# Queries of a self attention by seven block products of 128 tokens instead of eight

## The chip, the cores and the metric

One core of a Trainium2 chip runs the whole program in one launch. The metric is the device time of one execution in microseconds (us); several executions are timed and the median is given. A profile is one further execution taken with the hardware profiler; its times are from its own first instruction.

## What is computed

Sixteen elements of 256 tokens by 256 channels go through two transformer blocks. Each block has a self attention, a cross attention and a feed-forward part. All numbers are 32-bit floats. The change concerns the self attention of the first block (layer 0), cut here to what matters:

```python
def _attn(xq, ctx, wq, wkv, wo, bo):       # xq = ctx = adaptive layer norm of x, 256 tokens x 256
    q = _heads(xq @ wq)                    # wq: 256 x 1024, 16 heads of 64
    k, v = jnp.split(ctx @ wkv, 2, axis=-1)
    k = _heads(k)
    v = _heads(v)
    q = _rope(q, sq, cq)                   # rotary turn of each pair of channels
    k = _rope(k, sk, ck)
    sim = jnp.einsum('bhnd,bhmd->bhnm', q, k) * DH ** (-0.5)
    a = jax.nn.softmax(sim, axis=-1)
    o = jnp.einsum('bhnm,bhmd->bhnd', a, v)
    return o.transpose(0, 2, 1, 3).reshape(xq.shape[0], xq.shape[1], MID) @ wo + bo
```

## The kernel before

**Order.** The kernel writes out the instruction order of every engine by hand: what is called first stands first in each engine's queue. Six phases follow each other (layer 0 self, cross, feed-forward; the same for layer 1), each a loop over the 16 elements ("jobs"; `job["b"]` is the element, `job["p"]` the phase, 0 for the one changed). An attention job has two steps, s = 0 and s = 1. In each step two groups `u` = 2s and 2s + 1 of four heads are worked on. Step by step the kernel makes the queries and keys of the *next* step (`then`), the weighted sums of this one, and closes with `scores(i + 1)`: the products of queries and keys of the next step (`stage_s`, L657) into the eight PSUM banks, from which ScalarE takes the exponentials `pr` (L670).

**Products.** `product` (L82) is one 128 x 128 weight block times a moving operand, sent as four matmuls of 32 output columns. The trace keeps two records of each such matmul, so a product is eight records.

**Queries and keys before.** `stage_rotary` makes half a group: two products with 256 moving tokens for the keys and two for the queries, side by side in one bank. VectorE multiplies that bank by cosine and by sine (L614, tiles `m`), and after the second half GpSimd adds and subtracts the products (L622, tiles `qk`, 512 columns each for queries and keys together). A step has eight query products and eight key products. The four calls use banks 0, 1, 2 and 3 in turn.

**Values by seven.** The values of elements 2 to 15 are made in step s = 0 of the element before by seven block products in place of eight (a Strassen scheme in its Winograd form: two blocks of input channels by two blocks of tokens, and the same of the weights). `fold_tokens` (L532 to L535) makes the four sums of the input's blocks on GpSimd, `fold_value_weights` those of the weights, once. `value_part` puts the seven products (L82, 512 columns) into banks 4, 6 and 7 and collects them with ScalarE copies and VectorE additions: part 0 makes two products and copies bank 6 to bank 7 (L551); part 1 makes one product in bank 6 and one in bank 7 and copies both out (L555, L556); part 2 makes one more in bank 7, copies it out (L559) and adds on VectorE (L560); part 3 one in bank 7 (L563); part 4 one in bank 4 and an addition (L566).

**Around it.** `stage_t` (L676) adds the exponentials of two halves on VectorE, both inputs in SBUF; `stage_turn` (L682) and `stage_reduce` (L689) sum them over keys; `sum_up` makes the reciprocals and sends them through DRAM to `spread`. `layer0_sums` (L724) are the weighted sums of values, copied out by ScalarE (L731). On GpSimd `scale` (L713) multiplies them by the reciprocals and `fold_inner` (L1003) makes sums for the output product, `finish_folded`, which is 28 products of 128 moving columns (L82, operands `folded`, `raw`, `folded_w`, `wo_sa`), in step s = 1. The order of one step s = 0 with the values by seven was:

```python
rotary(then, 0, 0); rotary(then, 0, 1); sum_up(late, 5)
value_part(nxt, 0); stage_t(job, 1); stage_reduce(job, 0)
rotary(then, 1, 0); value_part(nxt, 1)
rotary(then, 1, 1); value_part(nxt, 2)
layer0_sums(job, 0, 5); value_part(nxt, 3)
layer0_sums(job, 1, 6); stage_turn(job, 1); value_part(nxt, 4); stage_reduce(job, 1)
```

Of the kernel before, what the change touches and what calls it, by code (L numbers as in the profile page):

```python
# [10 lines left out]
F32 = mybir.dt.float32  # L11
# [5 lines left out]
P = 128  # L17
# [26 lines left out]
def fast(ctx: ExitStack, tc: tile.TileContext, a: dict, out: bass.AP, flag):  # L44
# [19 lines left out]
    def bank(i, *inner):  # L64

        flat = banks[:, i, :]
        if len(inner) == 1:
            return flat[:, 0 : inner[0]]
        return flat[:, 0 : inner[0] * inner[1]].rearrange("p (a n) -> p a n", n=inner[1])
# [443 lines left out]
    def fold_value_weights(ph, eng):  # L513

        wv = ph["w"]["wv"]
        top, low = ([wv[:, k, r * 512 : (r + 1) * 512] for k in range(KC)] for r in range(2))
        sums = wtile([P, 4, 512], "wo", "sums_of_weights", 2)
        s2, s3, s4 = (sums[:, i] for i in range(3))
        eng.tensor_tensor(s3, top[0], low[0], ALU.subtract)
        eng.tensor_tensor(low[0], low[0], low[1], ALU.add)  # L520
        eng.tensor_tensor(s2, low[0], top[0], ALU.subtract)
        eng.tensor_tensor(s4, top[1], s2, ALU.subtract)
        ph["value_weights"] = {1: top[0], 2: top[1], 3: s4, 4: low[1], 5: low[0], 6: s2, 7: s3}

    def fold_tokens(job, eng):

        b = [[job["hT"][:, k, t * P : (t + 1) * P] for t in range(NT)] for k in range(KC)]
        t1, t2, t3, t4 = (
            tile[:, i, :] for tile in
            [wtile([P, 2, P], "bv", f"tokens{i}_{job['key']}", 2) for i in range(2)] for i in range(2)  # L530
        )
# [4 lines left out]
        job["tokens"] = {1: b[0][0], 2: b[1][0], 3: b[1][1], 4: t4, 5: t1, 6: t2, 7: t3}  # L536

# [3 lines left out]
    def value_part(job, part):  # L541
# [15 lines left out]
        elif part == 2:  # L557
            value_product(job, 7, 7)
            nc.scalar.copy(low2, chain)  # L559
            nc.vector.tensor_tensor(low2, bank(4, 512), low2, ALU.add)  # L560
        elif part == 3:
            value_product(job, 4, 7)
            nc.scalar.copy(low, chain)  # L563
        else:
            value_product(job, 3, 4)
            nc.vector.tensor_tensor(top2, bank(4, 512), top2, ALU.add)  # L566
# [604 lines left out]
    for i, (j, s) in enumerate(steps):  # L1171
# [123 lines left out]
        elif layer0:  # L1295
            then = attention(i + 1, 0)
            if leaving and s == 1 and nxt["kind"] == "ffn":
# [4 lines left out]
            if s == 0 and by_seven(nxt):  # L1302
# [14 lines left out]
                value_part(nxt, 2)  # L1317
                layer0_sums(job, 0, 5)
# [41 lines left out]
            else:  # L1360
                prepare_norm(third)
                prepare_context(third)
                prepare_input(after)
                if job["b"] == 0:
# [651 lines left out]
```

## Time and profile before

| what | value |
|---|---|
| five timed executions, median | 2162.98 us (2161.99 to 2165.33) |
| profiled execution: its time, its span | 2161.8 us, 2159.9 us |
| granted TensorE clock | 1.000 |
| TensorE matmuls busy | 2141.4 us, 50000 records |
| VectorE, ScalarE, GpSimd busy | 1654.6, 877.8, 1321.9 us |
| one element of the self attention, from scores to scores (184.73 to 225.18 us) | 40.45 us, TensorE busy for all of it |
| in that element: VectorE, ScalarE, GpSimd busy | 30.87, 13.30, 29.61 us |

Times are us from the start of the span unless marked ns. PE is TensorE's matmul side, PEld its weight loads, DVE VectorE, ACT ScalarE, POOL GpSimd. In the timeline a line has start, length, engine, source line, operation, output and inputs, and how many instructions were merged; in brackets the idle time before, and what ended it. A merged matmul line is longer than its share of TensorE, since matmuls overlap their successors: the distance between starts is what a group costs.

### The profile page before, as it was taken

The numbers are of one execution on the slowest core, as the hardware profiler recorded it, in microseconds if no ns is written. First come the engines' busy times: TensorE is split into PE (matmuls) and PEld (weight loads), VectorE is DVE, ScalarE is ACT, GpSimd is POOL, SyncE is SP. The second block draws the span as 40 slices with busy tenths as digits, with TensorE's granted clock in tenths as the row PEclk, the third lists the DMA queues.
The fourth block names the chain that finished last, engine by engine and source line by source line (L and its number), as shares of the span: only waits on it lengthen the run. The fifth ranks groups of instructions, "written<-read, shape, count | busy, mean of one in ns | idle before, by whom it ended". The sixth has DMA issues, their size and how long they took to land.

```text
span 2159.9 us, 109747 instructions
## 1 busy us (share of the span) xinstructions
PE 2141.4 (99%) x50000; PEld 1409.7 (65%) x50000; DVE 1654.6 (77%) x3008; ACT 877.8 (41%) x1376; POOL 1321.9 (61%) x1234
## 2 busy tenths in 40 slices
PE   9999999999999999999999999999999999999998
PEld 5666666666666666666666667887556556656787
DVE  6777777777787888888888777764777777778875
ACT  3333333333323332333323333443666666664442
POOL 5767767767767877686776766661322223236673
PEclk9999999999999999999999999999999999999999
DMA  5110010110133221211212023220211232223221
GB/s 195 26 42 23 25 41 22 25 41 23 29 84 93 74 60 35 58 44 44 58 35 60 26 75 93 52 50 22 64 41 43 53 95 63 60 49 81 70 66 39
DMA packets 307027, 117.65 MB, mean 54 GB/s; under 512 B 243364, under 2 KB 289784, under 8 KB 306424
## 3 DMA queue, kind: packets, MB, share of 16 engines
q1 hardware_dynamic: 306008, 110.02, 20.1%
q8 instruction: 393, 6.44, 1.2%
q14 instruction: 82, 0.67, 0.1%
q10 hardware_dynamic: 544, 0.52, 0.1%
HBM read 77.14 MB, written 33.29 MB: 51 GB/s over the span
## 4 chain that ended last, share of the span: by engine, by line
PE 95%; POOL 2%; DVE 1%; SPq 1%; DMA 1%; issue 1%; ACT 0%; POOLq 0%; DVEq 0%; ACTq 0%
PE banks L82 60%; PE banks L657 16%; PE banks L724 10%; PE banks L740 5%; PE banks L593 2%; PE banks L502 1%; POOL folded L926 0%; POOL folded_w L994 0%; POOL qk L622 0%; SPq L389 0%; DVE m L614 0%; SPq L379 0%; DVE xh L364 0%; POOL x L452 0%; DMA rows<-in_rows 0%
## 5 line engine op out<-in xcount | busy, mean ns | idle before, releaser
L670 ACT ACTIVATE pr<-banks 128x1024 f32<-128x1024 f32 x576 | 487.3, 938 | 422.9 <-PE banks L657 218.7
L622 POOL TENSOR_TENSOR qk<-m,m 128x512 f32<-128x512 f32 x256 | 378.7, 1500 | 213.3 <-DVE m L614 205.8
L614 DVE TENSOR_TENSOR m<-banks,rope 128x512 f32<-128x512 f32 x512 | 319.7, 678 | 35.0 <-PE banks L82 24.9
L676 DVE TENSOR_TENSOR both<-pr 128x1024 f32<-128x1024 f32 x128 | 170.0, 1328 | 104.0 <-ACT pr L670 102.0
L657 PE MATMUL banks<-qk 32*64 32x256 f32 x8192 | 239.4, 377 | 0.8 <-POOL qk L622 0.5
L724 PE MATMUL banks<-pr,v 128*32 128x256 f32 x4096 | 235.8, 379 | 0.0
L731 ACT COPY raw<-banks 128x512 f32<-128x512 f32 x128 | 75.1, 586 | 390.6 <-PE banks L724 384.6
L657 PEld LDWEIGHTS banks<-qk 32*64 32x64 f32 x8192 | 184.4, 131 | 59.9 <-issue 26.0
L724 PEld LDWEIGHTS banks<-pr,v 128*32 128x32 f32 x4096 | 133.4, 110 | 100.1 <-issue 16.8
L782 POOL TENSOR_TENSOR oT<-oT,spread 128x256 f32<-128x256 f32 x64 | 45.7, 736 | 206.7 <-DVE spread L781 206.7
L713 POOL TENSOR_TENSOR raw<-raw,spread 128x512 f32<-128x512 f32 x128 | 162.6, 1304 | 13.7 <-DMA spread<-sums_seen 13.5
L682 DVE STREAM_TRANSPOSE squares<-both 128x1024 f32<-128x1024 f32 x128 | 158.8, 1240 | 2.2
L689 DVE TENSOR_REDUCE rows<-squares 128x32 f32<-128x1024 f32 x128 | 155.2, 1212 | 1.7
L452 POOL TENSOR_TENSOR x<-x,bo_b 128x256 f32<-128x256 f32 x96 | 72.8, 778 | 121.6 <-DVE xh L364 121.6
L1003 POOL TENSOR_TENSOR folded<-raw,raw 128x512 f32<-128x512 f32 x90 | 142.9, 1615 | 2.4
L82 PE MATMUL banks<-hT,wk_sa 128*32 128x256 f32 x2048 | 134.7, 381 | 0.4 <-ACT hT L422 0.4
L740 PE MATMUL banks<-pr,wide_v 128*32 128x256 f32 x2048 | 134.4, 379 | 0.0
L82 PE MATMUL banks<-hT,wq_ca 128*32 128x256 f32 x2048 | 134.0, 379 | 0.0
L82 PE MATMUL banks<-hT,wq_sa 128*32 128x256 f32 x2048 | 133.9, 379 | 0.0
L356 POOL TENSOR_TENSOR rstd<-ve,neg_half 128x2 f32<-128x2 f32 x95 | 67.6, 712 | 101.5 <-DVE ve L354 97.7
L657 PE MATMUL banks<-q,k 32*64 32x256 f32 x4096 | 128.3, 381 | 0.2 <-issue 0.2
L957 DVE TENSOR_TENSOR x<-banks,x 128x256 f32<-128x256 f32 (+2 forms) x150 | 79.6, 531 | 62.6 <-PE banks L82 56.4
(246 smaller groups left out, 4044.8 us busy)
## 6 DMA issues: line engine op xcount, KB each, us to landing
turned<-blocks SPq DMA_DIRECT2D x380, 64.0 KB
fetched<-turned SPq DMA_DIRECT2D x380, 64.0 KB
spread<-sums_seen SPq DMA_DIRECT2D x128, 128.0 KB
x<-in_x SPq DMA_DIRECT2D x16, 256.0 KB
fetched_c<-turned_c SPq DMA_DIRECT2D x64, 64.0 KB
cT<-in_ctx_turned SPq DMA_DIRECT2D x16, 256.0 KB
out<-x SPq DMA_DIRECT2D x15, 256.0 KB
ctx<-in_ctx SPq DMA_DIRECT2D x16, 192.0 KB
```

What stands on the lines that cost most here:

```text
L82: nc.tensor.matmul(out[cut], lhsT[:, cut], rhs, start=start, stop=stop, **more)
L614: nc.vector.tensor_tensor(m, pq, rope[:, s : s + 1, :].to_broadcast([P, 2, N]), ALU.mult)
L622: nc.gpsimd.tensor_tensor(r, x, y, (ALU.subtract, ALU.add)[out])
L657: nc.tensor.matmul(banks[64 * g : 64 * g + 64, at + h, t * N : (t + 1) * N], lhs, rhs, start=(half == 0 and (t == 0 or job["layer"] == 1)) ...
L670: nc.scalar.activation(pr[:, one], sc[:, one], AF.Exp, scale=0.125 if job["layer"] == 0 else 0.25)
L676: nc.vector.tensor_tensor(both, pr[:, :, 0, :], pr[:, :, 1, :], ALU.add)
L682: nc.vector.transpose(job["squares"].rearrange("p b k -> p (b k)"), job.pop("both").rearrange("p h n -> p (h n)"))
L689: nc.vector.tensor_reduce(job["rows"][:, u, :], job.pop("squares"), AX.X, ALU.add)
L713: nc.gpsimd.tensor_tensor(part, part, spread[:, u : u + 1, :].to_broadcast([P, 2, N]), ALU.mult)
L724: nc.tensor.matmul(o[32 * h : 32 * h + 32, half, :], v[:, t, col : col + 32], pr[:, h, t, :], start=(t == 0), stop=(t == NT - 1),)
L740: nc.tensor.matmul(o[32 * h : 32 * h + 32], v[:, t, 4 * c + h, 32 * e : 32 * e + 32], pr[:, h, t, :], start=(t == 0), stop=(t == NT - 1),)
L1003: eng.tensor_tensor(folded[m], *sums[m])
```

## The change

The queries of elements 3 to 15 are made by the same seven-product scheme as the values: for each step, seven block products of a 256 x 256 part of `wq`, each over one block of 128 tokens (two calls of `product` with 128 moving columns). They use the input sums that the value products already have; `fold_tokens` keeps them in one tile of the pool `work` in place of two of `wpool`. `fold_query_weights` makes the sums of the weights on GpSimd, in step s = 1 of element 1 for one half of `wq` and of element 2 for the other, one of them in place. `query_part` collects the blocks in banks 0 and 2: `chain` and `low2` are the halves of bank 0, `top` and `top2` those of bank 2. ScalarE copies the chain three times (`copy` and two `keep`), VectorE adds twice. The keys keep their eight whole products per step, in banks 1 and 3. `rotate` turns keys (`which` = 1) and queries (`which` = 0) apart: two multiplications of 512 columns on VectorE as before, and two additions of 256 columns on GpSimd. The addition at the end of value part 2 is now a part of its own, "join". The order within the steps concerned is rewritten. It holds for 26 steps: (2, s = 1) to (15, s = 0), of which the twelve s = 0 steps of elements 3 to 14 hold the value products as well.

```diff
     def bank(i, *inner):
         flat = banks[:, i, :]
+        if not inner:
+            return flat
         if len(inner) == 1:
             return flat[:, 0 : inner[0]]
         return flat[:, 0 : inner[0] * inner[1]].rearrange("p (a n) -> p a n", n=inner[1])
...
         wv = ph["w"]["wv"]
         top, low = ([wv[:, k, r * 512 : (r + 1) * 512] for k in range(KC)] for r in range(2))
-        sums = wtile([P, 4, 512], "wo", "sums_of_weights", 2)
+        sums = ph["sums"] = wtile([P, 4, 512], "wo", "sums_of_weights", 2)
         s2, s3, s4 = (sums[:, i] for i in range(3))
         eng.tensor_tensor(s3, top[0], low[0], ALU.subtract)
         eng.tensor_tensor(low[0], low[0], low[1], ALU.add)
...
     def fold_tokens(job, eng):
         b = [[job["hT"][:, k, t * P : (t + 1) * P] for t in range(NT)] for k in range(KC)]
-        t1, t2, t3, t4 = (
-            tile[:, i, :] for tile in
-            [wtile([P, 2, P], "bv", f"tokens{i}_{job['key']}", 2) for i in range(2)] for i in range(2)
-        )
+        whole = work.tile([P, 2, N], F32, tag="cT", name=f"tokens_{job['key']}")
+        t1, t2, t3, t4 = (whole[:, i // 2, i % 2 * P : (i % 2 + 1) * P] for i in range(4))
         eng.tensor_tensor(t1, b[0][1], b[0][0], ALU.subtract)
         eng.tensor_tensor(t2, b[1][1], t1, ALU.subtract)
         eng.tensor_tensor(t3, b[1][1], b[0][1], ALU.subtract)
         eng.tensor_tensor(t4, b[1][0], t2, ALU.subtract)
         job["tokens"] = {1: b[0][0], 2: b[1][0], 3: b[1][1], 4: t4, 5: t1, 6: t2, 7: t3}
+    def queries_by_seven(then):
+        return then is not None and then[0]["p"] == 0 and then[0]["b"] > 2
+    def fold_query_weights(ph, s, eng):
+        if s == 0:
+            few = wtile([P, 4, N], "mod", "sums_of_query_weights")
+            ph["query_sums"] = [ph["sums"][:, 3, i * N : (i + 1) * N] for i in range(2)] + [few[:, i] for i in range(4)]
+        s2, s3, s4 = ph["query_sums"][3 * s : 3 * s + 3]
+        w = ph["w"][f"wq{s}"]
+        low, top = ([w[:, k, r * N : (r + 1) * N] for k in range(KC)] for r in range(2))
+        eng.tensor_tensor(s3, top[0], low[0], ALU.subtract)
+        eng.tensor_tensor(low[0], low[0], low[1], ALU.add)
+        eng.tensor_tensor(s2, low[0], top[0], ALU.subtract)
+        eng.tensor_tensor(s4, top[1], s2, ALU.subtract)
+        ph.setdefault("query_weights", []).append({1: top[0], 2: top[1], 3: s4, 4: low[1], 5: low[0], 6: s2, 7: s3})
+    def query_part(then, part):
+        job, s = then
+        chain, low2 = (bank(0)[:, i * N : (i + 1) * N] for i in range(2))
+        top, top2 = (bank(2)[:, i * N : (i + 1) * N] for i in range(2))
+        def block(place, m, start=False):
+            a = job["phase"]["query_weights"][s][m]
+            for half in range(2):
+                cut = slice(half * P, (half + 1) * P)
+                product(place[:, cut], a[:, cut], job["tokens"][m], start and half == 0, True, skip_group_check=True)
+        def keep(i):
+            job["kept"].append(wtile([P, N], "bv", f"kept{i}_{job['key']}_{s}", 2))
+            nc.scalar.copy(job["kept"][i], chain)
+        if part == 0:
+            job["kept"] = []
+            block(top, 1, True)
+            block(top2, 5)
+            nc.scalar.copy(chain, top)
+        elif part == 1:
+            block(top, 2)
+            block(chain, 6)
+            keep(0)
+        elif part == 2:
+            block(chain, 7)
+            keep(1)
+        elif part == 3:
+            nc.vector.tensor_tensor(low2, top2, job["kept"][1], ALU.add)
+        elif part == 4:
+            block(chain, 4)
+            block(top2, 3)
+        else:
+            nc.vector.tensor_tensor(top2, top2, job["kept"][0], ALU.add)
+    def keys(then, e, half):
+        job, s = then
+        at = (2 * e + half) * P
+        for k in range(2):
+            product(
+                bank(2 * e + 1, 2, N)[:, half, :], job["phase"]["w"][f"wk{s}"][:, k, at : at + P], job["kT"][:, k, :],
+                k == 0, k == 1,
+            )
+    def rotate(then, e, which):
+        job, s = then
+        key, u = job["key"], 2 * s + e
+        turns = []
+        for i in range(2):
+            m = work.tile([P, 2, N], F32, tag=f"m{i}", name=f"m{i}_{key}_{u}_{which}")
+            if which == 0:
+                view = m.rearrange("p t (h n) -> p t h n", h=2)
+                nc.vector.tensor_tensor(
+                    view, bank(2 * e).rearrange("p (t h n) -> p t h n", t=2, h=2),
+                    rope[:, i, :].rearrange("p (t o n) -> p t o n", t=2, o=1).to_broadcast([P, 2, 2, P]), ALU.mult,
+                )
+                turns.append([view[:, :, h, :] for h in range(2)])
+            else:
+                nc.vector.tensor_tensor(
+                    m, bank(2 * e + 1, 2, N), rope[:, i : i + 1, :].to_broadcast([P, 2, N]), ALU.mult
+                )
+                turns.append([m[:, h, :] for h in range(2)])
+        if u not in job["qk"]:
+            job["qk"][u] = [work.tile([P, 2, N], F32, tag="qk", name=f"qk_{key}_{u}_{i}", bufs=4) for i in range(2)]
+        cos, sin = turns
+        for i, r in enumerate(job["qk"][u]):
+            out = r[:, which, :].rearrange("p (t n) -> p t n", t=2) if which == 0 else r[:, which, :]
+            nc.gpsimd.tensor_tensor(out, cos[i], sin[1 - i], (ALU.subtract, ALU.add)[i])
     def value_product(job, m, at, start=False):
         product(bank(at, 512), job["tokens"][m], job["phase"]["value_weights"][m], start, True, skip_group_check=True)
...
         elif part == 2:
             value_product(job, 7, 7)
             nc.scalar.copy(low2, chain)
+        elif part == "join":
             nc.vector.tensor_tensor(low2, bank(4, 512), low2, ALU.add)
         elif part == 3:
             value_product(job, 4, 7)
...
                     fold_input(jobs[j + 1 : j + 3], nc.vector)
         elif layer0:
             then = attention(i + 1, 0)
+            if job["p"] == 0 and s == 1 and job["b"] in (1, 2):
+                weights_after = job["b"] - 1
+            else:
+                weights_after = None
             if leaving and s == 1 and nxt["kind"] == "ffn":
                 fold_input_weights(nxt["phase"], nc.gpsimd)
             if job["p"] == 0 and job["b"] == 0 and s == 1:
                 fold_value_weights(job["phase"], nc.gpsimd)
                 fold_weights(job["phase"], (1, 3))
-            if s == 0 and by_seven(nxt):
+            if queries_by_seven(then):
+                seven = s == 0 and by_seven(nxt)
+                if seven:
+                    fold_tokens(nxt, nc.gpsimd)
+                stage_t(job, 2 * s)
+                stage_turn(job, 2 * s)
+                for half in range(2):
+                    keys(then, 0, half)
+                rotate(then, 0, 1)
+                query_part(then, 0)
+                if s == 1:
+                    fold_inner(late, nc.gpsimd, 7, 6)
+                else:
+                    sum_up(late, 5 if seven else 6)
+                if make_mod:
+                    make_mod["mod"] = make_mod["make_mod"](6)
+                for half in range(2):
+                    keys(then, 1, half)
+                if seven:
+                    value_part(nxt, 0)
+                query_part(then, 1)
+                stage_t(job, 2 * s + 1)
+                stage_reduce(job, 2 * s)
+                rotate(then, 1, 1)
+                if seven:
+                    value_part(nxt, 1)
+                else:
+                    layer0_sums(job, 2 * s, 4)
+                query_part(then, 2)
+                if seven:
+                    stage_turn(job, 2 * s + 1)
+                    query_part(then, 3)
+                    value_part(nxt, 2)
+                else:
+                    query_part(then, 3)
+                    stage_turn(job, 2 * s + 1)
+                    layer0_sums(job, 2 * s + 1, 5)
+                query_part(then, 4)
+                rotate(then, 0, 0)
+                if seven:
+                    value_part(nxt, "join")
+                query_part(then, 5)
+                rotate(then, 1, 0)
+                if leaving and s == 0:
+                    load_phase(job["p"] + 1, "last")
+                if seven:
+                    layer0_sums(job, 0, 5)
+                    value_part(nxt, 3)
+                    layer0_sums(job, 1, 6)
+                    value_part(nxt, 4)
+                stage_reduce(job, 2 * s + 1)
+            elif s == 0 and by_seven(nxt):
                 fold_tokens(nxt, nc.gpsimd)
                 stage_t(job, 0)
                 stage_turn(job, 0)
...
                 value_part(nxt, 1)
                 rotary(then, 1, 1)
                 value_part(nxt, 2)
+                value_part(nxt, "join")
                 layer0_sums(job, 0, 5)
                 value_part(nxt, 3)
                 layer0_sums(job, 1, 6)
...
                 prepare_norm(third)
                 prepare_context(third)
                 prepare_input(after)
+                if weights_after is not None:
+                    fold_query_weights(job["phase"], weights_after, nc.gpsimd)
                 if job["b"] == 0:
                     fold_weights(job["phase"], (4, 6, 7) if job["p"] == 0 else (1, 3, 4, 6, 7))
         else:
```

## The prediction

> **What bounds the kernel now.** I read the busy shares first, then the chain of waits, then the timeline of one element.
>
> ```profile
> PE 2141.4 (99%) x50000; PEld 1409.7 (65%) x50000; DVE 1654.6 (77%) x3008; ACT 877.8 (41%) x1376; POOL 1321.9 (61%) x1234
> PE 95%; POOL 2%; DVE 1%; SPq 1%; DMA 1%; issue 1%; ACT 0%; POOLq 0%; DVEq 0%; ACTq 0%
> ```
>
> TensorE sets the end: it is 95% of the chain, and between two `scores` of the self attention it never stops. So a matmul saved there is time saved, and a wait put there is time lost, each in full. The price of a matmul is the distance between starts (timeline of TensorE, one step s = 1):
>
> ```profile
> 168.12 1.07 PE L82 MATMUL banks<-hT,wk_sa 128*32 128x256 f32 x16
> ...
> 175.05 3.64 PE L724 MATMUL banks<-pr,v 128*32 128x256 f32 x64
> 178.50 1.93 PE L82 MATMUL banks<-wo_sa,folded 128*32 128x128 f32 x64
> 180.25 1.93 PE L82 MATMUL banks<-folded_w,raw 128*32 128x128 f32 x64
> 181.99 2.80 PE L82 MATMUL banks<-folded_w,folded 128*32 128x128 f32 x96
> 184.73 3.71 PE L657 MATMUL banks<-qk 32*64 32x256 f32 x128
> ```
>
> From 168.12 to 175.05 stand 128 records of 256 columns: 54.1 ns each. From 180.25 to 181.99 stand 64 of 128 columns: 27.2 ns, half as much.
>
> **What it saves.** A step loses 8 query products of 8 records, 64 x 54.1 = 3.46 us, and gains 7 blocks of 2 products, 112 x 27.2 = 3.05 us: 0.416 us saved, in 26 steps 10.8 us. Bounds: at exactly half of 54.1 it is 0.43; at 28.5 ns, the dearest row (181.99 to 184.73, with the hand-over to another shape), 0.27. So 7.0 to 11.3 us; I take 10.8, since the middle row is undisturbed.
> The Trainium skill, page "TensorE: Matmul & The Clock Gate", section "Back-to-back issue gap", speaks against it: a sustained stream of weight load and matmul costs about 81 ns at 128 columns and 131 ns at 512, far from a quarter, because the loads set the pace. Interpolating those to 98 ns at 256 (an estimate from that page), the 56 matmuls in place of 32 would cost 1.4 us more per step and 36 us in all. The rows above, with the same 32-column weights in this program, show a half, so I don't take it.
>
> **What it adds: a wait of TensorE in s = 0.** This is the main cost. In the changed order value part 1 (which ends with a product into bank 7) is followed by query part 2 (one block) and then by value part 2, which writes bank 7 again. That write must wait until ScalarE has copied bank 7 out. Before, two groups of `rotary` stood between:
>
> ```profile
> 155.75 1.04 PE L82 MATMUL banks<-sums_of_weights,tokens 128*32 128x512 f32 x8
> 156.61 1.05 PE L82 MATMUL banks<-hT,wk_sa 128*32 128x256 f32 x16
> 156.91 0.59 ACT L556 COPY v<-banks 128x512 f32<-128x512 f32 x1 [0.33 <-PE banks L82]
> 158.34 1.04 PE L82 MATMUL banks<-sums_of_weights,tokens 128*32 128x512 f32 x8
> ```
>
> Call the end of part 1 on TensorE B (here 156.61). The copy starts at B + 0.30 and ends at B + 0.89; cover was 1.73 us (158.34 - 156.61), now it is one block, 16 x 27.2 = 0.435. How soon TensorE goes on after a release, an early wait shows:
>
> ```profile
> 69.87 1.44 POOL L532 TENSOR_TENSOR tokens<-hT 128x128 f32<-128x128 f32 x1
> 71.37 1.06 PE L82 MATMUL banks<-wv_sa,tokens 128*32 128x512 f32 x8 [2.31 <-POOL tokens L532]
> ```
>
> 69.87 + 1.44 = 71.31, so 0.06. Part 2 starts at B + 0.95: a wait of 0.51 us. Late next is query part 4: its first product waits for the addition of part 3 on VectorE, which waits for the second `keep` on ScalarE, queued behind the 0.59 us copy. The trace has no ScalarE copy of 128 x 256, no addition of that shape back into PSUM; the nearest:
>
> ```profile
> L752 ACT ACTIVATE oT<-banks,mask 128x256 f32<-128x256 f32 x64 | 32.8, 512 | 0.0
> L846 ACT ACTIVATE g<-banks,cols 128x256 f32<-128x256 f32 x52 | 21.8, 471 | 51.7 <-PE banks L82 45.7 <-POOL folded L926 6.0
> L1018 DVE TENSOR_TENSOR x<-banks,x 128x256 f32<-128x256 f32 x30 | 12.5, 418 | 0.0
> L452 POOL TENSOR_TENSOR x<-x,bo_sa 128x256 f32<-128x256 f32 x32 | 24.1, 775 | 49.4 <-DVE xh L364 49.4
> L622 POOL TENSOR_TENSOR qk<-m,m 128x512 f32<-128x512 f32 x256 | 378.7, 1500 | 213.3 <-DVE m L614 205.8 <-PE banks L82 4.9 <-PE banks L724 1.5
> ```
>
> 0.89 + 0.47 (keep) + 0.06 + 0.42 (addition) + 0.06 = B + 1.90; part 2's product of 0.865 ends at B + 1.81. Another 0.09. In all 0.60 us per step, x 12 = 7.2 us. Bounds: 0.51, if only the first wait binds, to 0.78, if VectorE comes to the addition late because one 0.74 us GpSimd operation held it up: 6.1 to 9.4.
>
> **A narrow place in s = 1.** Here 1.73 us of `layer0_sums` stand between parts 2 and 4, so part 4 is due 9.10 us after the step's start (1.73 + 0.87 + 1.73 + 0.87 + 1.73 + 0.44 + 1.73). ScalarE's keep ends at about 8.25 (part 2 ends at 7.37; the copy of the sums comes first, to 7.82, then 0.47 less overlap). VectorE: the second `both` started 5.47 after the step's start, with four `m` ahead of it; now two are ahead, 1.23 less, so 4.24, then 1.13 to the reduction, 1.26 to the next multiplications, 1.27 for these: free at 7.9. The addition ends at 8.73, released by 8.79: 0.31 to spare, and VectorE alone could be 0.72 late. What can make it late:
>
> ```profile
> 167.65 4.75 POOL L1003 TENSOR_TENSOR folded<-raw,raw 128x512 f32<-128x512 f32 x3
> 168.50 1.51 DVE L676 TENSOR_TENSOR both<-pr 128x1024 f32<-128x1024 f32 x1 [0.91 <-ACT pr L670]
> 173.59 1.20 DVE L676 TENSOR_TENSOR both<-pr 128x1024 f32<-128x1024 f32 x1
> 173.81 3.38 POOL L622 TENSOR_TENSOR qk<-m,m 128x512 f32<-128x512 f32 x2 [0.75 <-DVE m L614]
> ```
>
> `both` met `folded` and took 0.3 more than alone, and three `folded` took 4.75 against 3 x 1.27: the two engines exclude each other for such operations. GpSimd now comes to `scale` and `folded` some 1.9 us later (its last query sums wait for query part 5), so both `both` of the step meet it, each at up to one operation (1.27 us). Least 0, most 1.5 us per step. After the first meeting they run in step: transpose and two multiplications take 2.43 us, two `folded` 2.54, so the second wait should be about 0.1. I take 0.1 us x 13 = 1.3 us.
> The Trainium skill, "SBUF — State Buffer", section "Who interferes with whom", has the same exclusion, for the whole instruction, for a VectorE instruction with two SBUF inputs; it would exempt the new additions, which read PSUM and SBUF. No row of this trace has them, so that is open.
>
> **Costs at nothing.** ScalarE's three copies (1.4 us a step) and VectorE's two additions (0.84) fall into idle time outside the two chains above (13.3 and 30.9 us busy of 40.45). GpSimd: 16 sums of 0.74 (median of L452) in place of 8 of 1.29 (median of L622, two took 2.54 at 160.09) are 1.5 us more per element, against 10.8 idle. The scores of s = 1 need its third pair: s = 0's last pair ends at B + 7.8 (first query block of part 4 at B + 2.3, VectorE from 2.55 for 1.3 + 0.69 + 0.42 + 1.3, two sums of 0.74); then come `scale` 5.0, `folded` 5.7 with two meetings, `rstd` 0.7, three pairs 4.5, `folded` 2.5, so B + 26.2; TensorE comes there at B + 27.6 (7.9 to the scores, 3.64 for them, 9.97 to the end of part 4, 6.1 for `finish_folded`). Cover gone at 1.4 us. The weight sums, 4 x 0.74 = 3.0 us once in each of two steps, delay `tokens`, whose first sum ends at 188.69 and is used at 192.77, 4.1 us later; without that cover 1 to 3 us once. DMAs keep their number and order; loading the next `wq1`, `wk1` in (15, s = 0) waits some 3 us longer on the SP queue and the fetches behind it with it, 20 us before use.
>
> **Sum.** -10.8 + 7.2 + 1.3 = -2.3 us. Profiled span 2159.9 to 2157.6; its time was 2161.8, the median 2162.98, so 2160.7 for the median.
>
> **Rivals.**
> 1. *The waits don't bind* (ScalarE releases bank 7 within the 0.435 us): -10.8, 2152.2 us. Against: 0.89 us from end to end of the copy in every such step. Chance 0.12.
> 2. *VectorE falls out of step with GpSimd in s = 1*: the second `both` arrives just after a third `folded` has begun (2.43 against 2.54 leaves 0.1) and waits 1.27. With the 0.5 of the first it passes the 0.72 by 1.07 us, x 13 = 13.9: -10.8 + 7.2 + 13.9 = +10.3, 2173.3 us. It is slower by over 0.2% from 0.61 us a step on. For: the margin is thin. Chance 0.18.
> 3. *GpSimd becomes the bound*: should a 256-column sum cost as much as one of 512 (1.29), three pairs are 3.3 us longer and the one before 1.1; 3.0 beyond the cover, x 12 = 36, so about 2197 us. Against: L452 at 0.775. Chance 0.04.
>
> **Numbers.** Forecast 0.66, from -10.8 + 6.1 = -4.7 to -10.8 + 9.4 + 4 = +2.6: 2158.3 to 2165.6. About 0.2% (4.3 us) is what a measurement of this kernel tells from no change. Of the forecast's 0.66 some 0.13 lies below that, 0.50 within, 0.03 above. Faster 0.12 + 0.13 = 0.25; same 0.50; slower 0.03 + 0.18 + 0.04 = 0.25. The range 2155 to 2172 leaves out rival 1, rival 3 and a part of rival 2.
>
> **What would show it.** Query matmuls of 128 columns at 27 ns a record. Idle time of TensorE of about 0.5 us ahead of value part 2, ended by ScalarE, twelve times; small idle ahead of part 4, ended by VectorE. A step s = 0 from the first keys to `scores` of 16.7 to 16.8 us (16.57 before), s = 1 of 16.3 (16.61). It is wrong if s = 1 has waits of over 0.3 us, if `scores` waits for `qk`, or if bank 7 is free in time.

## The result and the profile after

| kernel | median us (lowest to highest), runs | ratio to before, 95% interval |
|---|---|---|
| before | 2162.98 (2159.80 to 2166.54), 41 | |
| changed | 2167.25 (2162.22 to 2169.53), 21 | 1.002 [1.0014, 1.0026] |

The changed kernel is slower by 4.3 us where -2.3 were forecast: inside the range, on the other side. Its profiled execution took 2168.5 us (span 2166.5, granted clock 0.997). Its page, the head and the chain by engine:

```profile
span 2166.5 us, 112523 instructions
...
PE 2140.8 (99%) x51248; PEld 1437.4 (66%) x51248; DVE 1683.2 (78%) x3060; ACT 904.1 (42%) x1454; POOL 1344.9 (62%) x1346
...
PE 83%; POOL 8%; DVE 4%; issue 3%; DMA 1%; ACT 0%; SPq 0%; DVEq 0%; POOLq 0%; ACTq 0%
```

TensorE's share of the chain fell from 95% to 83%; GpSimd (2% to 8%) and VectorE (1% to 4%) took most of the difference. Its waits (engine, what it waited for: us in total, times, longest):

```profile
PE banks L84 <- ACT v L647: 4.6, 11, 0.4
PE banks L84 <- DVE inner L932: 4.0, 1, 4.0
PE banks L84 <- DVE banks L585: 2.8, 12, 0.3
PE banks L84 <- POOL tokens L532: 2.3, 1, 2.3
```

The first is the predicted wait of s = 0 (value part 2 behind ScalarE's copy). The third is in s = 1 and just as common; L585 is the addition of query part 3. The second stands once, where layer 1's feed-forward begins, outside everything that was changed; in the kernel before it was 1.4 us. The last is in both kernels.

Step times show how it adds up (us from scores to scores):

| step | before | changed | predicted |
|---|---|---|---|
| (2, 1), the first one changed | 20.25 | 19.86 | |
| s = 0 with the values, 12 of them | 20.21 | 20.43 | +0.18 |
| s = 1, the others | 20.25 | 20.29 | -0.32 |
| (15, 0), without values | 19.51 | 19.11 | |

The table gives medians. Summed over the 26 steps, the twelve s = 0 lose 2.6 us, the twelve s = 1 lose 0.6, and the two others gain 0.39 and 0.40: +2.4 us. The rest of the 6.6 us between the two spans, by the marks that both traces share: 0.3 ahead of the first scores, 2.0 in step (1, 0), most of it at a lower clock behind 72 us, 3.5 where layer 1's feed-forward begins, less 1.6 in the phases between. The medians are only 4.3 apart: the profile of before had no lower clock ahead of its end (1.000; its timed runs 0.9989 on average), that of the changed kernel a lower one than its timed runs (0.997; 0.9979).

One element on TensorE (timeline of the changed kernel), s = 0 and then s = 1:

```profile
199.40 0.62 PE L84 MATMUL banks<-tokens,sums_of_query_weights 128*32 128x128 f32 x16
200.44 1.07 PE L84 MATMUL banks<-sums_of_weights,tokens 128*32 128x512 f32 x8 [0.41 <-ACT v L647]
201.29 0.65 PE L84 MATMUL banks<-tokens,wq_sa 128*32 128x128 f32 x16
...
218.50 1.91 PE L816 MATMUL banks<-pr,v 128*32 128x256 f32 x32
220.65 0.65 PE L84 MATMUL banks<-tokens,wq_sa 128*32 128x128 f32 x16 [0.24 <-DVE banks L585]
```

In s = 0 the query block at 199.40 costs 0.435, so value part 2 was due at 199.84 and started 0.60 later (the bracket shows less, since a merged line's modelled end lies behind its last start). In s = 1 the weighted sums at 218.50 cost 1.73, so part 4 was due at 220.23 and started 0.42 later.

What makes part 4 late, all engines one element earlier, same kernel:

```profile
171.48 4.63 POOL L1095 TENSOR_TENSOR folded<-raw,raw 128x512 f32<-128x512 f32 x3
...
174.86 2.34 DVE L768 TENSOR_TENSOR both<-pr 128x1024 f32<-128x1024 f32 x1
...
178.13 0.38 ACT L570 COPY kept<-banks 128x256 f32<-128x256 f32 x1
178.25 1.27 DVE L618 TENSOR_TENSOR m<-banks,rope 128x512 f32<-128x512 f32 x2
179.12 2.53 POOL L1095 TENSOR_TENSOR folded<-raw 128x512 f32<-128x512 f32 x2
179.44 0.42 DVE L585 TENSOR_TENSOR banks<-banks,kept 128x256 f32<-128x256 f32 x1
...
179.92 0.65 PE L84 MATMUL banks<-tokens,wq_sa 128*32 128x128 f32 x16 [0.23 <-DVE banks L585]
```

`both` takes 1.2 us alone (173.59 in the profile before); here 2.34, to 177.20. The same timeline in narrower windows parts the three `folded`; the second and the third:

```profile
173.59 1.29 POOL L1095 TENSOR_TENSOR folded<-raw,raw 128x512 f32<-128x512 f32 x1
...
174.83 1.28 POOL L1095 TENSOR_TENSOR folded<-raw,raw 128x512 f32<-128x512 f32 x1
```

`both` came 0.03 us after the third had begun, and its 2.34 us are what is left of that operation, to 176.1, and about 1.1 of its own. From there VectorE is late in all that follows, and comes to the addition at 179.44, though its operand `kept` was there at 178.51.

### The profile page after: what moved, and what is told of

Its sections match the earlier page's. It is cut to its first block, busy times and chain, and to the rows that moved or that the text cites. A ratio compares the mean times of both kernels' runs of the same rounds, so it can differ in the third digit from the quotient of the medians.

```text
span 2166.5 us, 112523 instructions
## 1 busy us (share of the span) xinstructions
PE 2140.8 (99%) x51248; PEld 1437.4 (66%) x51248; DVE 1683.2 (78%) x3060; ACT 904.1 (42%) x1454; POOL 1344.9 (62%) x1346
## 4 chain that ended last, share of the span: by engine, by line
PE 83%; POOL 8%; DVE 4%; issue 3%; DMA 1%; ACT 0%; SPq 0%; DVEq 0%; POOLq 0%; ACTq 0%
PE banks L84 55%; PE banks L749 14%; PE banks L816 6%; PE banks L832 5%; POOL raw L805 3%; POOL folded L1095 2%; PE banks L685 1%; POOL qk L627 1%; PE banks L504 1%; DVE m L618 1%; DVE m L612 1%; DVE rows L781 1%; POOL qk L714 0%; DMA spread<-sums_seen 0%; DMA fetched<-turned 0%
## 5 line engine op out<-in xcount | busy, mean ns | idle before, releaser
L714 POOL TENSOR_TENSOR qk<-m,m 128x512 f32<-128x512 f32 x152 | 220.7, 1473 | 125.6 <-DVE m L706 124.1
L768 DVE TENSOR_TENSOR both<-pr 128x1024 f32<-128x1024 f32 x128 | 180.8, 1413 | 96.4 <-ACT pr L762 94.8
L627 POOL TENSOR_TENSOR qk<-m,m 128x256 f32<-128x256 f32 x208 | 161.1, 798 | 88.3 <-DVE m L612 54.3
L706 DVE TENSOR_TENSOR m<-banks,rope 128x512 f32<-128x512 f32 x304 | 189.6, 678 | 22.7 <-POOL qk L714 10.6
L358 POOL TENSOR_TENSOR rstd<-ve,neg_half 128x2 f32<-128x2 f32 x95 | 82.6, 870 | 103.9 <-DVE ve L356 100.5
L84 PE MATMUL banks<-hT,wk_sa 128*32 128x256 f32 x2048 | 126.1, 383 | 0.0
```

Of the source, the lines that this page charges most:

```text
L84: nc.tensor.matmul(out[cut], lhsT[:, cut], rhs, start=start, stop=stop, **more)
L627: nc.gpsimd.tensor_tensor(out, cos[i], sin[1 - i], (ALU.subtract, ALU.add)[i])
L706: nc.vector.tensor_tensor(m, pq, rope[:, s : s + 1, :].to_broadcast([P, 2, N]), ALU.mult)
L714: nc.gpsimd.tensor_tensor(r, x, y, (ALU.subtract, ALU.add)[out])
L768: nc.vector.tensor_tensor(both, pr[:, :, 0, :], pr[:, :, 1, :], ALU.add)
```

## The experiments

Times are medians; "step" is from scores to scores in that kernel's profile. All edits are to the changed kernel unless they say before.

**Which step loses.** `s1_only` makes the queries by seven only where no values are made, `s0_only` only where they are:

```diff
-            if queries_by_seven(then):
+            if queries_by_seven(then) and not (s == 0 and by_seven(nxt)):   # s1_only
+            if queries_by_seven(then) and s == 0 and by_seven(nxt):         # s0_only
```

> Queries by seven only in the 14 steps that hold no value products (13 steps s = 1 and the last s = 0); the twelve s = 0 steps with value products go back to whole query products. Theory A (in s = 1 VectorE's second `both` waits behind GpSimd's `folded`, because the change made GpSimd later in s = 0): with s = 0 as before GpSimd is early again, the wait ahead of query part 4 is below 0.15 us, a step s = 1 takes 19.9 us from scores to scores in place of 20.25, and the kernel is about 5 us faster than before. Rival B (the wait comes from ScalarE's copies and VectorE's additions of the query parts themselves, wherever GpSimd stands): s = 1 stays at 20.2 to 20.3 us and the kernel is within 1 us of before.

> Queries by seven only in the twelve s = 0 steps with value products, all s = 1 steps with whole products. The step s = 0 has no other engine in doubt: its 0.6 us wait ahead of value part 2 stays, 20.43 us against 20.21, +2.6 us in twelve steps. Theory A expects s = 1 with whole products at 20.25 or a little less or more by no part 4 to wait: the kernel +2 to +3 us against before. Rival C (the loss against before is the half-clock stretches, not the steps): step times equal to before within 0.05 us, and a loss only where the granted clock is below 1.

Both edits leave the in-place sum of the query weights as it is, so the whole query products that come after it multiply a block of `wq` that already holds a sum. Those queries are not the right ones, and the two kernels serve for times alone.

`s1_only`: 2160.77 us, ratio 0.9991 [0.9982, 1.0]; s = 1 is 19.85. Alone, it saves the whole 0.40 per step: the second `both` (175.31, 1.25 us) meets no `folded`, and part 4 doesn't wait. So the order of s = 1 alone doesn't make the lateness; it takes the changed s = 0 ahead of it. The kernel is 2.4 us faster than before in the same runs, though, where about 5 were expected: its profile loses 1.2 us to a wait for those in-place sums (`wq_sa`) in step (3, 0) and 1.7 to a lower clock near 72 us. `s0_only`: 2167.75 us, 1.002 [1.0011, 1.0029]; s = 0 is 20.43 as in the full change, s = 1 20.25 as before. It is 4.6 us slower than before, where 2 to 3 were expected; its profile has stretches of lower clock near 72 and 1976 us.

**The wait of s = 0.** `wide_gap` puts the first weighted sums between query part 3 and value part 2:

```diff
                 if seven:
                     stage_turn(job, 2 * s + 1)
                     query_part(then, 3)
+                    layer0_sums(job, 0, 5)
                     value_part(nxt, 2)
...
                 if seven:
-                    layer0_sums(job, 0, 5)
                     value_part(nxt, 3)
```

> The changed kernel with the first weighted sums (`layer0_sums(job, 0, 5)`, 1.73 us of TensorE) moved from behind query part 4 to between query part 2 and value part 2 in the s = 0 steps. If the 0.6 us wait there is ScalarE's copy of bank 7 and the addition behind it, it is gone: s = 0 takes 19.8 to 19.9 us in place of 20.43, 12 x 0.6 = 7.2 us. But GpSimd's last pair of s = 0 then ends some 1.5 us after the scores have begun, so s = 1 may lose: theory A expects the wait ahead of part 4 in s = 1 to move within 0 to 1.2 us. If s = 1 stays as it is: 7 us faster than the changed kernel, 3 us faster than before. Rival D (something else ends the wait, such as the weight loads after a semaphore): s = 0 falls by less than 0.3 us.

2173.13 us, 1.0049 [1.0035, 1.0062]: a miss. Keys to scores fell from 16.79 to 16.31 us: the 0.6 ahead of value part 2 is gone, and 0.1 came back ahead of part 3. But the step became 21.26. Its timeline:

```profile
183.95 1.29 DVE L612 TENSOR_TENSOR m<-banks,rope 128x512 f32<-128x512 f32 x2 [2.22 <-POOL qk L627]
...
188.34 0.42 DVE L1116 TENSOR_TENSOR x<-banks,x 128x256 f32<-128x256 f32 x1
...
188.82 1.98 PE L749 MATMUL banks<-qk 32*64 32x256 f32 x62 [0.31 <-DVE x L1116]
```

VectorE idles 2.22 us for the tiles `m`, which GpSimd reads late; its residual additions slide back, and the scores stop half way for the bank of the last one. One wait was exchanged for a longer one, in the scores that follow s = 1.

**The narrow place of s = 1.** `late_turn` moves two multiplications behind the addition:

```diff
-                rotate(then, 1, 1)
                 if seven:
+                    rotate(then, 1, 1)
                     value_part(nxt, 1)
...
                     query_part(then, 3)
+                    rotate(then, 1, 1)
                     stage_turn(job, 2 * s + 1)
```

> The changed kernel with the second keys' multiplications (`rotate(then, 1, 1)`) of the s = 1 steps moved behind VectorE's addition of query part 3, so that VectorE comes to that addition 1.27 us earlier; nothing else. Theory A (VectorE, held up 1.2 us by GpSimd at the second `both`, is what part 4 waits for): the wait of 0.42 us in s = 1 is gone, s = 1 takes 19.85 to 19.9 us in place of 20.29, 13 steps give 5.4 us, the kernel is 1 to 2 us faster than before. Rival B (ScalarE's `keep` is late): nothing changes, s = 1 stays at 20.29. The lock itself stays: the second `both` still takes about 2.3 us.

2163.31 us, 0.9999 [0.999, 1.0008]: 3.9 us under the changed kernel, but level with before, where 1 to 2 us less were expected. Its timeline:

```profile
173.06 2.34 DVE L768 TENSOR_TENSOR both<-pr 128x1024 f32<-128x1024 f32 x1
...
176.74 0.43 DVE L585 TENSOR_TENSOR banks<-banks,kept 128x256 f32<-128x256 f32 x1 [0.21 <-ACT kept L570]
...
177.71 0.62 PE L84 MATMUL banks<-tokens,wq_sa 128*32 128x128 f32 x16
```

`both` loses the same 1.2 us, but nothing waits: the addition comes as soon as `kept` does, and s = 1 is 19.85. So it is VectorE's lateness at this one addition that costs 0.44 per step. What kept the time up stands outside these steps: the 4.0 us for `inner` are there too, and the mean clock of the timed runs was 0.998.

**Together.** `three_moves` is both moves, and `fold_inner(late, nc.gpsimd, 7, 6)` of s = 1 behind that `rotate`:

> Wide gap (first weighted sums between query part 2 and value part 2) and late turn (second keys' multiplications behind the addition of part 3) together, and in s = 1 GpSimd's `fold_inner(late, 7, 6)` moved behind its second pair of key sums, so that VectorE's last multiplications, which wait for that pair to free their buffers, need not wait for it. The wide gap alone took the 0.6 us out of s = 0 but lost 1.3 us in the scores, which waited for VectorE's last additions to x (L1116), pushed back by those multiplications. If that chain over GpSimd is the cause: no wait of the scores on L1116, s = 0 at 19.9 to 20.0 us, s = 1 at 19.85 us, 8 to 9 us less than before by steps, 2155 us. If not (GpSimd is simply too late in s = 0): s = 0 stays near 21.2 us, some 2171 us.

2157.03 us, 0.9964 [0.9952, 0.9977]; s = 0 is 19.94, s = 1 19.85. With `folded` later the second `both` takes 1.22 us, GpSimd has the query sums out of the way in time, and the wait that sank `wide_gap` is gone (0.3 us for L1116 in the whole run, 3.4 there). It beats both kernels.

**The rest of the shift.** In both kernels TensorE waits 2.3 us for `tokens` in step (1, 0). `tokens_first` and `before_tokens` move the keys' weight sums, which stand ahead of them on GpSimd, into that step; `three_and_tokens` is that on top of `three_moves`:

```diff
+                if job["b"] == 1:
+                    fold_weights(job["phase"], (4, 6, 7))
...
-                if job["b"] == 0:
-                    fold_weights(job["phase"], (4, 6, 7) if job["p"] == 0 else (1, 3, 4, 6, 7))
+                if job["b"] == 0 and job["p"] > 0:
+                    fold_weights(job["phase"], (1, 3, 4, 6, 7))
```

> The changed kernel with that move of `fold_weights` alone. Steps account for +2.4 us of the changed kernel's +4.3; the mean granted clock of its timed executions was 0.9979 against 0.9989 of before, 0.001 or 2 us. Theory E (the rest is the clock, which falls after waits of over 2 us near elements 1 and at the start of the feed-forward part, by chance of place and not by the changed steps): 2.3 us for the wait and 1 to 2 us for the clock are gained, 2163 to 2164 us, mean clock 0.9985 or more. Rival F (the changed steps themselves lower the clock): 2.3 us gained and the clock stays at 0.998.

> The kernel before with the same move. Its wait for `tokens` is the same 2.31 us: 2.3 us gained, and up to 1 us for the clock (0.9989 before): 2160 us. Theory E expects the changed kernel and before to differ by 2.4 to 3 us with this wait gone from both; rival F by 4 us or more.

> The same, with the last three sums of the output weights (`fold_weights(4, 6, 7)`, 3.75 us of GpSimd) moved from the end of element 0 to behind the tokens' sums of the next step. In every profile so far TensorE waits 2.31 us for `tokens` there, and in four of five profiles of changed kernels the granted clock then falls to about 0.6 over 4 us. Theory: wait and fall are gone, 2.3 us and some 1.3 us more than three_moves.

2166.02 (1.0005 [0.9996, 1.0014]), 2159.82 (0.9986 [0.9977, 0.9994]) and 2154.85 us (0.9961 [0.9948, 0.9974]). The wait is gone in all three. But `tokens_first` missed its 2163 to 2164, and changed minus before is now 6.2 us, more than the 2.4 of the steps and than the 2.4 to 3 of theory E. These two profiles differ by 2.1 us behind the self attention, by 1.0 ahead of layer 1's feed-forward and by 5.9 at the end. So nearly 5 us are lost there. Its beginning, in the timeline of the changed kernel and then of the one before:

```profile
1972.03 1.27 POOL L1018 TENSOR_TENSOR folded<-g 128x512 f32<-128x512 f32 x1
...
1972.48 1.09 DVE L931 TENSOR_TENSOR inner<-hT,hT 128x256 f32<-128x256 f32 x1 [1.27 <-ACT hT L424]
...
1973.68 1.30 DVE L932 TENSOR_TENSOR inner<-hT,inner 128x256 f32<-128x256 f32 x1
...
1975.04 3.64 PE L84 MATMUL banks<-inner,input_w_L_xcond_b 128*32 128x256 f32 x32 [4.02 <-DVE inner L932]
```

```profile
1968.26 0.43 DVE L839 TENSOR_TENSOR inner<-hT,hT 128x256 f32<-128x256 f32 x1 [0.19 <-ACT hT L422]
...
1968.79 0.42 DVE L840 TENSOR_TENSOR inner<-hT,inner 128x256 f32<-128x256 f32 x1
1968.88 1.47 POOL L926 TENSOR_TENSOR folded<-g 128x512 f32<-128x512 f32 x1
...
1969.27 1.93 PE L82 MATMUL banks<-inner,input_w_L_xcond_b 128*32 128x256 f32 x32 [1.41 <-DVE inner L840]
```

Against GpSimd's first `folded` the input `hT`, and with it the first addition, comes 1.07 us later in the changed kernel (0.45 behind its start instead of 0.62 ahead). The two additions then meet it and the next one and take 2.4 us instead of 0.85. It is the collision of s = 1 once more. And the 32 matmul records behind the wait take 3.64 us where the kernel before takes 1.93: about half speed.

`after_again` is the changed kernel a second time; the three `turned` kernels move the normalization and the transposes of element 4, with their transfers, behind the folded output weights:

```diff
-            if s == 1 and b > 0 and third is not None:
+            if s == 1 and b > (0 if layer0 else 1) and third is not None:
                 prepare_norm(third)
...
                             prepare_input(one, nc.scalar)
+                        prepare_norm(third)
```

> The changed kernel once more, as it is, for a second profile. Theory G (2.4 us of the loss stand in the changed steps, and 3 to 4 us where layer 1's feed-forward begins: the additions of `inner` come so late there that TensorE waits 4.0 us instead of 1.4 and then runs at a lower granted clock): the profile shows a wait of 3.5 to 4.0 us for `inner` again, a clock window under 0.8 behind it, and the median is 2166 to 2168 us. Rival H (that wait is an accident of single executions and belongs to neither kernel): the wait is another one, 1 to 2.6 us, and the clock stays at 1.000 there.

> The changed kernel with one thing moved, in layer 1's feed-forward, element 1: the normalization and transposes of element 4 (prepare_norm) and their four `turned` transfers stand in its third step, behind the folded output weights and the inputs of elements 2 and 3, instead of ahead of its second; the queue then carries the last `fetched` transfers of element 3 without them. Theory G: the wait for `inner` falls from 4.0 to under 2 us, no window of lower clock stands behind it, and the time is 3 to 4 us under the changed kernel's, 2162.5 to 2164.5 us. Rival H: nothing that matters, 2166 to 2168 us. If the wait stays at 4.0 us, the transfers of element 4 are not what makes `inner` late.

> The kernel before with the same move, to see that the move itself brings little where `inner` is not late. Both theories: the wait there is 0.5 to 1.5 us and the time is 2161 to 2163.5 us. Changed kernel minus this one, with the move in both: theory G 1.5 to 3 us (the changed steps alone), rival H 4 us or more.

> The kernel with three moves in the steps and the token sums ahead of the keys' folded weights, and the same move in layer 1's feed-forward on top. Theory G: 3 to 4 us under the 2154.9 us of that kernel, 2150.5 to 2152.5 us. Rival H: 2154 to 2155.5 us.

`after_again`: 2166.68 us, 1.0016 [1.0007, 1.0024], with the 4.0 us again, so it belongs to the kernel. `after_turned`: 2166.76, 1.0017 [1.0008, 1.0025]; wait 3.4. `before_turned`: 2164.26, 1.0004 [0.9995, 1.0013]; 2.1. `best_turned`: 2154.52, 0.996 [0.9947, 0.9972]; 2.0. The expectation of the move missed: the transfers of element 4 aren't what delays `hT`.

`after_fold`, `before_fold` and `best_fold` (on `three_and_tokens`) move GpSimd's `folded` instead, behind its bias additions of element 5:

```diff
-                if done is not None:
+                if done is not None and (layer0 or b != 2):
                     fold_hidden(done, nc.gpsimd, 5, 6, 7, 3)
...
                 prepare_norm(third)
+                if b == 2 and not layer0:
+                    fold_hidden(done, nc.gpsimd, 5, 6, 7, 3)
```

> The changed kernel with one thing moved, in layer 1's feed-forward, element 2: GpSimd's four `folded` sums of element 0 stand behind its additions of element 5's output bias, and so behind VectorE's four additions of `inner`, instead of ahead of them. Theory G2 (the inputs of element 3 come about 1 us late there, and VectorE's additions then meet GpSimd's sums: 1.09 and 1.30 us a piece where the kernel before has 0.43 and 0.42): the two additions take 0.42 to 0.70 us each, the wait for `inner` falls from 4.0 to 2.3 to 2.8 us, and the time is 1 to 3 us under the changed kernel's: 2164 to 2166 us; a new wait for `folded` of up to 1 us may take some of it back. Rival H2 (the late inputs alone decide): the additions' time changes little or the wait stays at 3.5 us or more, 2166 to 2168 us.

> The kernel before with the same move. In its profile the additions of `inner` start 0.6 us ahead of GpSimd's first sum, so both theories expect nothing from it but a possible wait for `folded`: 2162 to 2164.5 us, the wait for `inner` 1 to 2 us. Changed kernel minus this one, with the move in both: G2 2 to 3.5 us, H2 4 us or more.

> The kernel with three moves in the steps and the token sums ahead of the keys' folded weights (2154.85 us, a wait for `inner` of 4.0 us), with the same move on top. Theory G2: a wait of 2.3 to 2.8 us and 2152 to 2154 us. Rival H2: 2154 to 2155.5 us.

The timeline of `after_fold`:

```profile
1975.09 0.43 DVE L931 TENSOR_TENSOR inner<-hT,hT 128x256 f32<-128x256 f32 x1 [1.21 <-ACT hT L424]
...
1975.62 0.42 DVE L932 TENSOR_TENSOR inner<-hT,inner 128x256 f32<-128x256 f32 x1
...
1976.10 1.93 PE L84 MATMUL banks<-inner,input_w_L_xcond_b 128*32 128x256 f32 x32 [2.43 <-DVE inner L932]
```

The additions are back at 0.43 and 0.42 us, the wait at 2.4, and the matmuls behind it run at full speed (1.93). The three times are 2167.42 (1.0012 [1.0003, 1.0021]), 2161.24 (0.9992 [0.9983, 1.0001]) and 2153.60 (0.9955 [0.9941, 0.9969]). The collision is settled by the trace, but the first median didn't fall: 6.2 us between the first two, as the rival had it. The runs of `after_fold` lie in two groups, five of 2162 to 2165 us and six of 2167 to 2169.5, and its profile has the lower clock behind the wait for `tokens`. So `after_both` and `before_both` have that move and the one of the token sums:

> The changed kernel with the two moves outside the changed steps together: the token sums ahead of the keys' folded weights in step (1, 0), and GpSimd's folded sums of element 0 behind its bias additions in layer 1's feed-forward. Theory G3 (the changed steps cost 2.4 to 2.7 us, the late inputs of layer 1 another 1 to 1.5 us; the rest of what the medians showed is a lower clock behind the two long waits, which half of the executions have): no window of lower clock before the end, a mean clock of the timed runs of 0.999 or more, and 2161.5 to 2164 us. Rival H3 (the changed kernel loses more elsewhere): 2165 us or more.

> The kernel before with the same two moves. Both theories: 2157.5 to 2160.5 us (2159.8 us with the one and 2161.2 us with the other). Changed kernel minus this one, with both moves in each: G3 2.5 to 4.2 us, H3 5 us or more.

2162.68 (0.9995 [0.9986, 1.0004]) and 2158.79 us (0.9983 [0.9974, 0.9992]): 3.9 us apart, inside the 2.5 to 4.2 of its theory, and no second group. One detail missed: `after_both` still waits 2.9 us for `inner` (1.3 in the other) and has a window of 0.74 behind it.

## Why the prediction was wrong

The frame held: TensorE sets the end, and both the saving and the waits went to the time in full.

1. *The saving.* 0.416 us per step was right: 0.40 in (15, 0), and 0.40 in s = 1 wherever nothing was late. A 128-column query record costs 27.2 ns, as taken from the row of `folded_w`.
2. *The wait in s = 0.* 0.60 was right in size, though made differently: 0.60 at value part 2 (0.51 reckoned), none at part 4 (0.09 reckoned). The step moved by +0.22 against +0.18.
3. *The narrow place in s = 1* is the step that failed: 0.1 us a step taken, 0.44 measured (20.29 against 19.85) in twelve steps, 5.3 us instead of 1.3. These 4.0 us are most of the 4.7 by which the 26 steps missed (+2.4 for -2.3), and enough to turn their sign. "After the first meeting they run in step" was right, and the conclusion from it wrong. It compared 2.43 us of VectorE with 2.54 of GpSimd and let the second `both` come 0.1 us before the second `folded` ended; it came 0.03 us after the third had begun, and waited for all of it. That is the mechanism of rival 2, with its wait (1.2 us; 1.27 there) but not its price: 0.42 past the due time instead of 1.07 (1.05 by its own terms, 1.27 + 0.5 - 0.72), because VectorE reached the addition 9.05 us after the step's start, where 7.9 + 0.5 + 1.2 make 9.6. `late_turn` shows that this lateness is the whole loss of the step, `s1_only` that it takes a late GpSimd.
4. *Costs at nothing.* GpSimd's 256-column sums took 0.73 us each, so rival 3 fell, and `scores` never waited for `qk` in the changed steps (in `wide_gap` its cover, the time that TensorE needs until it gets there, was used up). The sums of the query weights cost at most 0.16 us (step (3, 0), which follows them, 20.59 against 20.43). What this part didn't look at was anything behind the self attention: where layer 1's feed-forward begins the changed kernel lost 3.2 to 4.9 us in three profiles, by a late input, a collision that the one before escapes by 0.6 us, and the lower clock behind the wait.
5. *The clock.* The sum had no term for it. Mean over the timed runs: 0.9989 before, 0.9979 changed; 0.001 is 2.2 us. It isn't a fixed cost of the change: `after_again` had 0.9987, against 0.9992 for the kernel before in the same runs.
6. *An open point.* The prediction left open whether an addition that reads PSUM and SBUF waits for GpSimd, since its trace had none of the new ones. But that trace has 28 rows of the same kind with 512 columns, beside a busy GpSimd; the last section shows one.

What stays open: why `hT` comes 1 us later there. The instructions around it are the same, the four transfers behind it aren't the cause (`after_turned`), and other orders of the same changed steps had 1.1 us (`wide_gap`) or 4.0 (`late_turn`). The 1.5 us that `after_both` keeps beyond the 2.4 aren't parted into late inputs and clock. And whether the lower clock behind the wait for `tokens` is more frequent in the changed kernel (7 of its 9 profiles with that wait, none of 3 of the kernel before) or fell so by chance wasn't settled.

## What to carry to other kernels

Where two engines exclude each other, cover is not a mean: ask at which operation of the other one an instruction arrives, and price the loss at a whole operation unless the arrival is known to a tenth of a microsecond. Two moves in one kernel can each look useless or harmful and pay together (`wide_gap` +10.0 us and `late_turn` +0.2, with a third move -6.7, against before in the same runs), since each takes away the wait that the other runs into. When two kernels differ by more than the changed code shows, line up the marks of both traces to the end: half or more of what parted these profiles arose 1300 us behind the last changed instruction.

## What was not expected of the hardware

*Exclusion.* A VectorE addition with both inputs in SBUF waits for the GpSimd operation that is running: `both` 2.34 us against 1.22, `inner` 1.09 and 1.30 against 0.43 and 0.42. The new additions with one input in PSUM don't: at 179.44 in the changed kernel one took 0.42 us while two `folded` ran, which took their usual 2.53. The value additions of the kernel before, also PSUM and SBUF, showed it already; this one began in the midst of four GpSimd operations and took 0.69 us, as all 28 did:

```profile
162.58 4.99 POOL L713 TENSOR_TENSOR raw<-raw,spread 128x512 f32<-128x512 f32 x4
...
164.61 0.69 DVE L566 TENSOR_TENSOR v<-banks,v 128x512 f32<-128x512 f32 x1 [2.71 <-PE banks L82]
```

The Trainium skill, "SBUF — State Buffer", section "Who interferes with whom", says just that, and these rows agree.

*The clock falls after short waits.* Windows of the changed kernel and of the one before (length; busy us and instructions of PE, PEld, DVE, ACT, POOL; granted clock; DMA share, GB/s):

```profile
72.00:76.00 4.00, 4.00 (x40) 1.82 (x44) 0.72 (x1) 0.00 (x0) 3.74 (x5) 0.59 0.62 173
1972.00:1976.00 4.00, 0.96 (x12) 0.51 (x16) 3.41 (x3) 2.14 (x5) 3.92 (x4) 0.74 0.23 42
1976.00:1980.00 4.00, 4.00 (x44) 1.87 (x40) 3.72 (x7) 0.00 (x0) 2.72 (x4) 0.50 0.70 215
1980.00:1984.00 4.00, 4.00 (x104) 2.92 (x100) 1.38 (x2) 2.73 (x6) 0.32 (x1) 0.90 0.68 182
```

```profile
72.00:76.00 4.00, 4.00 (x61) 1.78 (x56) 1.42 (x3) 0.59 (x2) 3.15 (x4) 1.00 0.64 197
```

Both kernels wait 2.31 us just before 72 us; this time only one is slowed behind it. Over all 19 profiles: behind a wait of 1.1 to 1.4 us for `inner` the clock never fell (6 profiles), behind one of 2.9 to 4.0 always (8); behind those of 2.0 to 2.7 in 2 of 5, and behind the 2.31 for `tokens` in 7 of 12. The fall at 72 us costs 1.6 us (0.41 of 4), that behind `inner` in this profile 2.9 (half of the 0.96 us of matmuls ahead of 1976, 0.50 of the next 4 us and 0.10 of the 4 behind those). So a wait of 2 to 3 us costs itself and, in part of the executions, nearly as much again.
The Trainium skill, "TensorE: Matmul & The Clock Gate", section "Part 1: The HAM clock gate", puts the fall to half rate after an idle window of about 3.4 us that runs freely; the half rate agrees with 0.50 and with the 3.64 us for 1.93, but here 2.31 us of idle were enough in 7 of 12 profiles.
